# Four chains of sampled attention on one ring of four PSUM banks, next to the banks of the feed-forward

## The chip, the cores and the metric

The kernel runs on one core of a Trainium2 chip. The metric is the device time of one execution in microseconds. Instructions of an engine stand in one queue and start in that order. PE is the engine of the matmuls, PEld its weight loads, DVE, ACT and POOL are the vector, scalar and general engines, and SP issues most of the DMAs. PE writes into PSUM, which has eight banks of 128 x 512 float32.

## What is computed

The reference is a network of four layers on a batch of four sequences of 1024 rows and 128 features. Each layer is an attention-like part and a feed-forward part, each followed by `layernorm(x + part(x))`. The change touches only layer 1:

- *Sampled attention* (16 heads of 8). From 35 sampled keys a measure is worked out for each query, and for each head the 35 queries with the largest measure are *chosen*. Only the chosen queries attend to all 1024 keys, by a softmax. All other rows of the output are the mean of the values. Then the output projection, the residual and the norm.
- *Feed-forward with two routes.* A shared expert for every row, and one of two experts per row by the sign of a gate, each of 128 to 512 to 128 features with a relu. Residual and norm follow.

Layer 2 (linear attention, mixture of experts) starts when layer 1 is done with the last batch.

## The kernel before

The program is written with generators. Each step of a batch (`l1_values`, `l1_chosen`, `l1_project`, `l1_ffn`) is one that yields between groups of instructions, and `weave` (line 52) goes round its generators in turn, one group of each. So the program order interleaves the batches. A scheduler then sets the order of each engine's queue when the program is built, from that program order, from the data and from the free buffers, with a model of time of its own. So the order of PE is fixed at build time, and on the chip a matmul that waits holds up all that stand behind it.

PSUM is handed out by `banks` (line 90). It makes one pool for each tag, with a number of banks; `bank(tag)` gives a function that takes the next tile of that pool. A pool is a ring: with four banks, the fifth tile needs one of the first four to have been read and given back. When the pools are replaced by others (a change of stage), a new pool's banks must have been given back by the old one.

The steps that the change moves, for a batch `b`:

- `l1_choose(1)` (line 574): finds the chosen queries of batches 2 and 3, with two transposes of the measure on PE, and five rounds of maximum (`t`), index search (`iu`) and replacement on DVE, each about 1.2 us. It then writes the indices (`idi`) to DRAM and reads them back as lists (`ix`). `l1_choose(0)` did the same for batches 0 and 1 a stage earlier.
- `l1_values(b)` (line 610): the mean of the values (`pvm`), written to all rows of the output in DRAM (`orows`), and the values themselves (`pv` to `vN`).
- `l1_chosen(b)` (line 637): five indirect DMAs on POOL gather the chosen rows (`xgs`); transposes on PE and two matmuls (`pqs`) make the queries, which DVE masks by head (`qs`). Then a loop of five blocks `j` of 112 queries: scores against 1024 keys in two tiles of 512 (`sc0`, `sc1`); the maximum of each on DVE (`smx`), and a bias from the two (`snm`); two exponentials on ACT with their sums (`esc`); eight transposes of 128 columns into two tiles (`pt`), copied to SBUF by ACT (`eT`); eight matmuls with the values (`pav`); scaling and masking on DVE (`o`); and an indirect DMA on POOL that scatters the block into `orows`. That is five PSUM tiles for each block: two scores, two transposes, one sum.
- `l1_project(b)` (line 744): when all five scatters have landed, SP reads `orows` back (`oL`). Then twice (for each half of the rows): transposes (`pt`), a copy with bias on ACT (`oT`), the output projection (`po`), the residual on DVE (`sp_r`), the norm (`norm_parts`, line 151), and transposes of the normed rows into `xT`.
- `l1_ffn(b)` (line 794): for each half, the gate (`pg`), and for three weights four matmuls with relu (`ph`, by turns on ACT and DVE, to `ht`) and four that add up in one bank (`po<-ht`). It needs `xT` of that half. Each half has 25 matmuls of 512 columns in the program, each of which the profile shows as two instructions. At its end stand a bias on ACT (`yT`), transposes, residual and norm.

`front` orders these. In a first stage it weaves `l1_choose(1)` with the chains of batches 0 and 1 (values, chosen, project). Each of these two chains has a pool of four banks (`c0`, `c1`). Then comes a change of stage: pools `c` (four banks), `f0` (three) and `o0` (one). The chains of batches 2 and 3 share `c`, and beside them goes the feed-forward of batches 0 and 1, one after the other, on `f0` and `o0`. After a second change, the feed-forward of batches 2 and 3 runs on `f0`, `o0`, `f1` and `o1`, and layer 2 follows.

Of the kernel before, what the change touches and what calls it, by code (L numbers as in the profile page):

```python
# [19 lines left out]
B, T, D = 4, 1024, 128  # L20
# [31 lines left out]
def weave(*gens):  # L52

    gens = list(gens)
    while gens:
        for g in gens[:]:
            if next(g, gens) is gens:
                gens.remove(g)


class Net:
# [786 lines left out]
    def front(self, ctx, w0, W, d, dp):  # L848

        tc = self.tc  # L850
        names = lambda n, s: [dp.tile(s, F32, name=f"{n}{b}", bufs=1) for b in range(B)]
        xd, orows = names("xd", [T, D]), names("orows", [T, D])
        ds = [dp.tile([2, 2, HU], I32, name=f"ds{i}", bufs=1) for i in range(2)]
        nb = self.const.tile([P, 4], F32, name="nbz")
        for i in range(2):
            self.nc.vector.tensor_scalar_mul(nb[:, i : i + 1], self.col(f"bz{i}"), -1.0)
            self.nc.vector.tensor_scalar_add(nb[:, 2 + i : 3 + i], self.col(f"bh{i}"), 0.5)
        with ExitStack() as right:
            with ExitStack() as left:
                sp = left.enter_context(tc.tile_pool(name="slot1", bufs=1))  # L860
                wp = left.enter_context(tc.tile_pool(name="slot2", bufs=2))
                with self.banks(g0=2, g1=2, g2=2, g3=2), tc.tile_pool(name="gru", bufs=4) as gp:
                    weave(
                        *(self.l0_gru(b, self.bank(f"g{b}"), self.wgru, nb, gp) for b in range(B))
                    )
                    self.l0_slots(W, sp)
                left.enter_context(self.banks(u=2, p0=3, p1=3))
                pu, pp = self.bank("u"), [self.bank(f"p{b % 2}") for b in range(B)]
                cp = right.enter_context(tc.tile_pool(name="spc", bufs=1, side="right"))
                qp = right.enter_context(tc.tile_pool(name="spq", bufs=2, side="right"))  # L870
                c = self.l1_load(cp)
                c["v"] = {}
                self.l1_gate(cp)
                route = lambda b: self.l0_route(b, pp[b], W, wp)
                read = lambda b, ps: self.l0_read(b, ps, W, wp, xd[b])
                measure = lambda b: self.l1_measure(b, pp[b], c, qp)
                weave(*(route(b) for b in range(B)))
                weave(self.l0_update(pu, W, wp))
                weave(
                    *(chain(read(b, pp[b]), measure(b)) for b in range(2)),  # L880
                    *(read(b, pu) for b in range(2, B)),
                )
                weave(self.l1_choose(0, pu, c, qp, ds[0]), measure(2), measure(3))
            w0.close()
            sp = right.enter_context(tc.tile_pool(name="sp2", bufs=2, side="right"))
            values = lambda b, ps: self.l1_values(b, ps, c, sp, orows[b])
            chosen = lambda b, ps: chain(
                self.l1_chosen(b, ps, c, sp, xd[b]), self.l1_project(b, ps, c, sp)
            )
            with self.banks(c0=4, c1=4):  # L890
                ps = [self.bank(f"c{i}") for i in range(2)]
                weave(
                    self.l1_choose(1, ps[1], c, qp, ds[1]),
                    *(chain(values(b, ps[b]), chosen(b, ps[b])) for b in range(2)),
                )
            fp = ctx.enter_context(tc.tile_pool(name="ff1", bufs=2))
            ffn = lambda b, i: self.l1_ffn(b, self.bank(f"f{i}"), self.bank(f"o{i}"), d, fp)
            with self.banks(c=4, f0=3, o0=1):
                pc = self.bank("c")
                weave(  # L900
                    *(chain(values(b, pc), chosen(b, pc)) for b in range(2, B)),
                    chain(ffn(0, 0), ffn(1, 0)),
                )
        ctx.enter_context(self.banks(f0=3, o0=1, f1=3, o1=1))
        return ffn(2, 0), ffn(3, 1)
# [1309 lines left out]
```

## Time and profile before

| what | us |
| --- | --- |
| median of 17 runs | 2275.1 |
| lowest and highest run | 2268.27, 2285.0 |
| the profiled execution | 2275.47 |
| its span, first to last instruction | 2273.7 |
| PE busy in the span | 1991.2 (88%) |
| DVE, ACT, POOL busy | 1351.0, 1194.1, 1024.0 |
| mean granted clock of PE | 0.934 of full speed |

The profile is of one execution. Times in its timeline count from the start of the span. The marks of the stretch that matters here are these starts:

| mark | us |
| --- | --- |
| first `pvm` of batch 0 | 233.48 |
| first gather (`xgs`) of batch 0 | 241.00 |
| first `sc` of batch 0 | 250.79 |
| first exponential of batch 0 | 257.82 |
| end of the last `pav` of batch 1 | 299.8 |
| `pvm` of batches 2 and 3 | 322.48 |
| first `pg` of the feed-forward of batch 0 | 328.50 |
| first `sc` of batch 2 | 332.50 |
| end of the last `pav` of batch 3 | 425.6 |
| first `pg` of the feed-forward of batch 2 | 465.55 |
| first matmuls of layer 2 (`pv<-wE`) | 598.7 |

How to read it: a busy PE is not PE at its peak, since matmuls are pipelined and their ends are modelled. So the start of one instruction to the start of the next says more than a duration. A wait is put down to the instruction that released it. Idle time of an engine that is not the bottleneck costs nothing by itself.

### The profile page before, as it was taken

Reading aid. Unit: us, or ns where it says so; the run is one execution under the profiler, and the core shown is the slowest. Engines: PE = TensorE matmul, PEld = TensorE weight load, DVE = VectorE, ACT = ScalarE, POOL = GpSimd, SP = SyncE. Lnnn points to the kernel's source line nnn. Section 1 sums busy time; section 2 is a strip of 40 time slices with the busy share of each in tenths; the row PEclk is TensorE's granted clock in tenths of the full one; section 3 lists DMA queues with packets and bytes.
Section 4 is the critical chain, followed back from the end, with each engine's and each line's share of the span. In section 5 each row is a group of like instructions: output and inputs, shape, how many; then the busy total and the mean of one; then the engine's idle time right before and its main releaser. Section 6 shows DMA issues by size and latency. Waiting matters only on the chain.

```text
span 2273.7 us, 46313 instructions
## 1 busy us (share of the span) xinstructions
PE 1991.2 (88%) x17788; PEld 1388.1 (61%) x17788; DVE 1351.0 (59%) x3668; ACT 1194.1 (53%) x2606; POOL 1024.0 (45%) x812
## 2 busy tenths in 40 slices
PE   6679889989999999999979876689899989998998
PEld 3456555544477777787868664346565656565666
DVE  7657743443455554655555565686777688776521
ACT  6533344322244444444565556466768786767443
POOL 5100320000123234234143329989798989879400
PEclk9668889989999999999999997899999999999999
DMA  3000110050000010031232066466776676776421
GB/s 107 0 24 15 38 40 1 19 175 0 1 3 2 3 37 24 18 88 41 80 82 83 17 176 210 124 181 193 199 213 178 182 186 187 196 186 180 108 61 51
DMA packets 138555, 211.09 MB, mean 93 GB/s; under 512 B 18596, under 2 KB 75933, under 8 KB 137950
## 3 DMA queue, kind: packets, MB, share of 16 engines
q1 hardware_dynamic: 126190, 173.87, 25.5%
q0 software_dynamic: 12144, 34.26, 7.2%
q8 instruction: 140, 2.29, 0.4%
q14 instruction: 81, 0.66, 0.1%
HBM read 160.29 MB, written 23.16 MB: 81 GB/s over the span
## 4 chain that ended last, share of the span: by engine, by line
PE 44%; DVE 13%; ACT 11%; issue 3%; DMA 2%; POOL 1%; SPq 0%; ACTq 0%; POOLq 0%; DVEq 0%
PE py L129 8%; PE ph L129 7%; PE po L1131 5%; PE pqk L129 5%; PE pa_m L129 4%; DVE db L1859 4%; PE kp_mo L129 3%; PE pr L1201 2%; PE pv L129 2%; PE pys L129 2%; ACT da L1858 1%; PE pt L133 1%; ACT hh L1985 1%; PE kp_mo L133 1%; ACT xN L176 1%
## 5 line engine op out<-in xcount | busy, mean ns | idle before, releaser
L1064 POOL TENSOR_TENSOR qt<-r_q,sb_c_turn 128x256 f32<-128x256 f32 (+1 forms) x256 | 164.6, 663 | 448.9 <-ACT r_q L1056 444.8
L1870 POOL TENSOR_TENSOR hc<-db,cn 128x1024 f32<-128x1024 f32 x128 | 316.3, 2504 | 62.6 <-PE pys L129 41.0
L129 PEld LDWEIGHTS py<-wh,hh 128*128 128x128 f32 x2048 | 252.8, 194 | 82.5 <-issue 46.7
L1854 POOL TENSOR_TENSOR db<-ud,bn 128x1024 f32<-128x1024 f32 x112 | 289.0, 2654 | 12.4 <-issue 9.9
L129 PE MATMUL py<-wh,hh 128*128 128x128 f32 x2048 | 260.2, 278 | 14.7 <-ACT hh L1985 7.1
L129 PE MATMUL ph<-xT,wh 128*128 128x512 f32 x512 | 255.4, 616 | 19.4 <-DVE h_acc L2001 5.1
L1985 ACT ACTIVATE hh<-ph,sb_cols 128x512 f32<-128x512 f32 x256 | 170.7, 681 | 124.4 <-PE ph L129 97.4
L1122 DVE TENSOR_TENSOR a<-pa_m,sb_c_near 128x256 f32<-128x256 f32 x256 | 96.5, 419 | 203.5 <-PE pa_m L129 203.5
L1079 ACT ACTIVATE kN<-kp_mo,sb_c_trig 128x128 f32<-128x128 f32 x448 | 130.2, 372 | 129.9 <-PE kp_mo L133 121.8
L1858 ACT ACTIVATE da<-dl,aneg 128x512 f32<-128x512 f32 x224 | 153.3, 689 | 79.7 <-DVE db L1859 78.8
L129 PE MATMUL pys<-hc,sb_c_ident 128*128 128x512 f32 x324 | 160.7, 626 | 20.3 <-POOL hc L1870 16.7
L1859 DVE TENSOR_TENSOR_SCAN db<-da,carry,db 128x512 f32<-128x512 f32 x128 | 157.1, 1265 | 12.8 <-ACT da L1858 9.9
L1859 DVE TENSOR_TENSOR_SCAN db<-da,db 128x512 f32<-128x512 f32 x128 | 149.3, 1204 | 9.2 <-POOL db L1854 5.2
L129 PEld LDWEIGHTS ph<-xT,wh 128*128 128x128 f32 x512 | 89.3, 195 | 100.4 <-issue 53.5
L2001 DVE SCALAR_TENSOR_TENSOR h_acc<-py,gt,h_acc 128x128 f32<-128x128 f32 x256 | 71.9, 342 | 130.2 <-PE py L129 130.2
L129 PE MATMUL pqk<-xT,wE 128*128 128x256 f32 x512 | 137.5, 392 | 8.3 <-ACT coT L1198 4.3
L129 PEld LDWEIGHTS pys<-hc,sb_c_ident 128*128 128x128 f32 x324 | 61.4, 202 | 83.9 <-issue 57.8
L129 PEld LDWEIGHTS pqk<-xT,wE 128*128 128x128 f32 x512 | 89.2, 194 | 22.0 <-DVE cv L1041 8.1
L1198 ACT COPY coT<-pt 128x512 f32<-128x512 f32 x64 | 37.6, 587 | 118.2 <-PE pt L133 118.2
L129 PE MATMUL po<-ht,wD 128*128 128x512 f32 x192 | 92.5, 594 | 0.0
L844 DVE TENSOR_SCALAR ht<-ph,sb_cols 128x512 f32<-128x512 f32 x48 | 35.7, 749 | 90.2 <-PE ph L129 90.1
L1131 PE MATMUL po<-cv,a 128*64 128x65 f32 x2048 | 88.3, 228 | 0.0
(453 smaller groups left out, 4275.0 us busy)
## 6 DMA issues: line engine op xcount, KB each, us to landing
wx<-in_wF SPq DMA_DIRECT2D x92, 384.0 KB, 3.4
bn<-rows SPq DMA_DIRECT2D x128, 256.0 KB, 4.8
cn<-rows SPq DMA_DIRECT2D x128, 256.0 KB, 4.4
wh<-in_wH SPq DMA_DIRECT2D x64, 512.0 KB, 3.7
hc<-hc POOLq DMA_DIRECT2D x47, 512.0 KB, 7.0
xrows<-zero SPq DMA_DIRECT2D x4, 1472.0 KB, 10.5
xg<-xrows SPq DMA_DIRECT2D x20, 256.0 KB, 3.6
yrows<-ys SPq DMA_DIRECT2D x20, 256.0 KB, 3.2
```

What stands on the lines that cost most here:

```text
L129: return self.nc.tensor.matmul(out=out, lhsT=lhsT, rhs=rhs, start=start, stop=stop)
L133: self.nc.tensor.transpose(out, in_, self.ident[0:n, 0:n])
L1064: nc.gpsimd.tensor_mul(u["qt"][:, m, a:], u["q"][:, a:], c2["turn"][:, m, o + a : o + 2 * P])
L1079: self.nc.scalar.activation(u["kN"][:, c, m, :], pk[:, c, :], AF.Copy, scale=trig[:, k, m : m + 1])
L1122: nc.vector.tensor_mul(u["a"][:, i, :, :], pa[i], self.c2["near"][:, None, :].to_broadcast([P, 2, P]),)
L1131: self.nc.tensor.matmul(out=u["po"][self.HALF[j], i, c, :], lhsT=lhsT, rhs=rhs, start=key not in u["begun"], stop=True, skip_group_check=True,
L1854: nc.gpsimd.tensor_mul(db, ud, bc[0])
L1858: nc.scalar.activation(da, dl[:, ec, :], AF.Exp, scale=aneg[:, j : j + 1])
L1859: nc.vector.tensor_tensor_scan(db[:, ec, :], da, db[:, ec, :], carry[:, ec, n : n + 1] if h else 0.0, ALU.mult, ALU.add,)
L1870: nc.gpsimd.tensor_mul(hc, db, bc[1])
L1985: nc.scalar.activation(ht, ph, AF.Relu, bias=self.col("h_b1", i=e * NK + k))
L2001: nc.vector.scalar_tensor_tensor(acc[:, c, :], py[:, c, :], gt[:, c, e : e + 1], acc[:, c, :], ALU.mult, ALU.add,)
```

## The change

Both stages become one, with the pools `c=4`, `f0=3`, `o0=1` from the start. `chosen_pair(0)` runs the chain of batch 0 and then that of batch 2, and `chosen_pair(1)` the chains of batches 1 and 3. `l1_choose(1)` and both pairs take all their PSUM tiles from the one ring `c`. When a chain has been written out to its end, its batch is put into `ready`, and `ffn_pair` begins with the feed-forward of a batch when it finds it there. The last stage is as it was.

```diff
-            with self.banks(c0=4, c1=4):
-                ps = [self.bank(f"c{i}") for i in range(2)]
-                weave(
-                    self.l1_choose(1, ps[1], c, qp, ds[1]),
-                    *(chain(values(b, ps[b]), chosen(b, ps[b])) for b in range(2)),
-                )
             fp = ctx.enter_context(tc.tile_pool(name="ff1", bufs=2))
             ffn = lambda b, i: self.l1_ffn(b, self.bank(f"f{i}"), self.bank(f"o{i}"), d, fp)
+            ready = set()
+
+            def chosen_pair(b):
+
+                for b in (b, b + 2):
+                    yield from values(b, pc)
+                    yield from chosen(b, pc)
+                    ready.add(b)
+
+            def ffn_pair():
+
+                for b in range(2):
+                    while b not in ready:
+                        yield
+                    yield from ffn(b, 0)
+
             with self.banks(c=4, f0=3, o0=1):
                 pc = self.bank("c")
                 weave(
-                    *(chain(values(b, pc), chosen(b, pc)) for b in range(2, B)),
-                    chain(ffn(0, 0), ffn(1, 0)),
+                    self.l1_choose(1, pc, c, qp, ds[1]),
+                    chosen_pair(0),
+                    chosen_pair(1),
+                    ffn_pair(),
                 )
```

## The prediction

> **What bounds the kernel now.** I read the page first: PE is busy for 88% of the span. The change touches one stretch of 232 us, so next I cut that stretch into parts with the view of busy time by window: the loop of chains 0 and 1 (257.8 to 299.8), their projection and the change of banks (to 328.5), the loop of chains 2 and 3 (332.5 to 425.6), and their projection (to 465.5). The columns are length, then busy time (and count) of PE, PEld, DVE, ACT, POOL, then the granted clock.
>
> ```profile
> 257.80:299.80 42.00, 40.74 (x276) 29.77 (x276) 26.05 (x77) 23.43 (x60) 17.71 (x19) 1.00 0.10 16
> 299.80:328.50 28.70, 18.08 (x113) 15.46 (x113) 12.49 (x58) 10.64 (x22) 5.81 (x4) 0.76 0.27 74
> 332.50:425.60 93.10, 90.00 (x388) 53.65 (x387) 38.00 (x111) 38.75 (x80) 8.47 (x9) 0.93 0.01 1
> 425.60:465.50 39.90, 33.29 (x123) 18.13 (x121) 20.07 (x79) 11.54 (x21) 0.94 (x1) 0.93 0.10 27
> ```
>
> The reader is to see that PE bounds the first loop and the third part, and that the second part is the hole: 10.6 of 28.7 us without PE work, at a clock of 0.76. The view of waits for PE in that part names the longest:
>
> ```profile
> PE pt L133 <- DMA oL<-orows: 5.4, 1, 5.4
> ```
>
> Third, the timeline of PE in the first loop, where each chain has four banks (start, length, what; the idle time before it in brackets):
>
> ```profile
> 279.14 1.95 PE L129 MATMUL sc<-kT,qs 128*112 128x512 f32 x4
> 280.93 0.93 PE L133 MATMUL pt<-sb_c_ident,esc 112*128 112x112 f32 x8
> 281.70 1.67 PE L129 MATMUL pav<-vN,eT 128*112 128x32 f32 x16
> 283.20 1.95 PE L129 MATMUL sc<-kT,qs 128*112 128x512 f32 x4
> 284.99 0.88 PE L129 MATMUL pav<-vN,eT 128*112 128x32 f32 x8
> 285.71 0.96 PE L133 MATMUL pt<-sb_c_ident,esc 112*128 112x112 f32 x8
> 286.91 0.97 PE L129 MATMUL pav<-vN,eT 128*112 128x32 f32 x8 [0.24 <-ACT eT L712]
> 287.72 1.95 PE L129 MATMUL sc<-kT,qs 128*112 128x512 f32 x4
> ```
>
> Scores (sc) of one chain stand between the transposes (pt) and sums (pav) of the other: the chains are half a round apart, and each one's softmax hides behind the other's matmuls. A round of both takes 287.72 - 279.14 = 8.6 us with 0.24 us idle.
>
> Fourth, the timeline of the loop of chains 2 and 3, which already share one ring of four. This round has almost no feed-forward work in it:
>
> ```profile
> 413.22 2.81 PE L129 MATMUL sc<-kT,qs 128*112 128x512 f32 x6
> ...
> 416.24 0.69 ACT L695 ACTIVATE esc<-sc,snm 112x512 f32<-112x512 f32 x1 [3.64 <-DVE snm L691]
> ...
> 419.11 0.69 ACT L695 ACTIVATE esc<-sc,snm 112x512 f32<-112x512 f32 x1 [0.19 <-DVE ln_mv L161]
> ...
> 419.94 1.27 PE L133 MATMUL pt<-sb_c_ident,esc 112*128 112x112 f32 x8 [1.59 <-ACT esc L695]
> ```
>
> Here both chains run in step: all scores first, then both wait for the exponentials, the second chain's 2.87 us after the first's.
>
> **The change, part by part.** Each queue's order in the changed program, as built, shows the same instructions but two more ACT table loads (2531 ACT instructions for 2529). What changes is order, and five terms follow.
>
> **1. The loop of chains 0 and 1, +13 us.** Ten tiles a round (two sc, two pt, one pav a chain) on four banks force the in-step order: in the changed order PE has sc A, sc A, sc B, sc B, pt A x2, pt B x2, pav A, pav B. Work of a round from the rows above: four sc at 0.44 x 2, four pt at 0.39, two pav at 1.5, or 8.1 us. Waits, with sc A's start as 0: the first maximum starts 1.13 later (279.14 to 280.27 in the trace), the second maximum is late because the rest of the last pav B now stands between the two sc A, so exp A starts at about 4.0; pt A may follow an exponential by 1.0 (258.50 to 259.52), at 5.05, while PE is free at 4.25: 0.8 idle. On DVE the row for chain B's bias is behind chain A's sum of exponentials, so exp B starts at about 6.45 and pt B at 7.45, with PE free at 6.1: 1.35. Two waits of 0.3 for second halves are left. 8.1 + 2.75 = 10.8 us a round. The measured in-step rounds agree: 358.70 to 370.50 is 11.8 with 0.86 of feed-forward and 0.43 of yT transposes in it, so 10.5.
>
> The start is later as well. PE now has chain 0's pqs behind the fourth gathered block of chain 1, which it transposes at 253.73; before, pqs ran at 247.77. On DVE the choice of batches 2 and 3 goes ahead of most of qs: pqs at 254.0, qs 0.69 later, then a maximum 1.22, two qs 0.5 each, an index search 1.28, a qs, and two reductions with small casts between, which brings the first exponential to about 261.5 for 257.82. Since exp A is 4.0 into a round, round 1 counts from 257.5. The last pav ends at 257.5 + 4 x 10.8 + 12 = 312.7, against 299.8: +13. Bounds: +2 if a round stays at 8.57, +26 if it takes 13.5, as it would with PE at half clock in half of it (sc pairs then take 1.92 instead of 1.02).
>
> POOL now has the ten gathers for chains 2 and 3 ahead of all scatters. They wait for the choice, which now ends near 261 (at 268.83 before), with 4.3 from there to the first gather (268.86 to 273.12) and 12.4 for ten. The scatters start at about 278; the first buffer of four is wanted again in the third round, past 286. I cost this at nothing.
>
> **2. The first projection, -4 us.** The wait of 5.4 for oL stays: nothing in PE's new order stands in it. The first xT is copied at 314.75, 15 us after the last pav; there the feed-forward (pg, ph) now starts, instead of 28.7 us after it. But values, gathered blocks and pqs of chains 2 and 3 are put behind almost its whole first half. From the last pav to chain 2's first sc: before 32.7 us with 3 feed-forward matmuls at 0.86 in them, 30.1 without. After, 15.7, then 25 such matmuls (21.5), the values (3.9), the transposes and pqs (3.0) and 3.5 left of the projection: 47.6, or 26.1 without the 21.5. So -4; bounds -11 (all 10.6 idle filled) and 0.
>
> **3. The loop of chains 2 and 3, +1 us.** 50 feed-forward matmuls instead of 47, paid for in terms 2 and 4. Two rounds are unfilled in either order. The two table loads of 1.28, and exp of chain 3 behind a square root that waits for the feed-forward's statistics, give 0 to +4; I take 1.
>
> **4. The second projection, +8.5 us.** This is what is late next. Before, a half of feed-forward (25 x 0.86 = 21.5) runs inside 39.9 us, so the rest costs 18.4. In the new order the feed-forward of batch 1 has ended its first half before the first oL transpose, and its next half stands behind the whole projection. The cover is gone, and the chain scatter, oL, transpose, po, two normalisations runs bare, as the first one did: there the last xT was copied 26.3 us after the last pav, though values were in between (pv 3.74). I take 27: 27 - 18.4 = +8.5. Bounds 0 and +12.
>
> **5. Later layers, 0.** Up to the expert layers the order is the same; in the last layer some pairs swap. No row prices that; I allow 4 us either way, three scans of 1.27.
>
> Sum: 13 - 4 + 1 + 8.5 = +18.5. The profiled execution took 2275.47 us (span 2273.7, 1.8 outside it), and the median of 17 runs is 2275.1, so the same holds for both: **2294 us**.
>
> [...] After the waits of 1.30 and 1.59 us PE slowed (second view, a pair of sc at 1.92):
>
> ```profile
> 365.92 1.27 PE L133 MATMUL pt<-sb_c_ident,esc 112*128 112x112 f32 x8 [1.30 <-ACT esc L695]
> ...
> 370.50 1.92 PE L129 MATMUL sc<-kT,qs 128*112 128x512 f32 x2
> ```
>
> The granted clock was 0.57 from 370 to 380 us and 0.66 from 420 to 430. In the first loop, with waits of 0.24, it was 1.00. [...] By the rows the new loop may lose the clock in each round, up to the +26 of term 1 and a sum of +31.
>
> **Rivals.**
> - *The loop also loses its clock* (13.5 us a round): 26 - 4 + 1 + 8.5 = +31.5, 2307 us. For it: both unfilled in-step rounds were followed by a low clock. Against: sc rows recur every 11 us. 0.20.
> - *Faster*: the feed-forward fills the first hole entirely and the ring costs the loop nothing, since a bank comes free before PE reaches it. Then +2 - 11 + 1 + 3 (a tail half covered): -5, 2270 us. It decides at a round of 8.9 us or less. For it: ACT is busy for 23.4 and DVE for 26.0 of 42 us, so no other engine forces a longer round. Against: the measured in-step rounds. 0.08.
> - *Nothing to see*: rounds of 9.5 (+6), the hole half filled (-7), a tail at +3 and 1: +3, 2278. The holes only change places. 0.10.
> - The forecast: 2282 to 2303 us, 0.62.
>
> **How the numbers follow.** About 0.2%, 4.5 us, is what a measurement of this kernel can tell from no change. Faster by more than that: 0.08; within it: 0.10; slower: 0.62 + 0.20 = 0.82. The range leaves out the faster rival and the upper half of the clock rival: 2277 to 2309.
>
> **What would show it.** Right: in-step order in the first loop with PE waits for exp of 1 us or more, the last pav of chain 1 near 313, ph starting some 16 us after it, no ph between chain 3's last pav and its last xT, and the first pg of batch 2 near 484 instead of 465.55. Wrong: rounds under 9 us, or ph inside the second projection. A changed time in the layers after 620 us would have another cause.

## The result and the profile after

The changed kernel took 2306.5 us (median of 8 runs, 2301.82 to 2311.12); the kernel before took 2275.87 (46 runs). The ratio is 1.0132, interval 1.0115 to 1.0148: 30.6 us slower. The profiled execution took 2315.62 us (span 2313.8), 9 us above the median; a second profiled execution of the changed kernel, taken with the experiments, took 2299.06, 7 below it. Both are used here, as *changed* and *changed again*.

Busy time by window of the changed kernel, with the columns of the prediction's first fence (length, PE, PEld, DVE, ACT, POOL, clock, DMA share, GB/s): the first loop, the first projection, the feed-forward that now stands between, the second loop, the second projection.

```profile
260.70:323.70 63.00, 56.88 (x281) 38.83 (x279) 23.65 (x73) 24.35 (x61) 17.82 (x19) 0.79 0.07 11
323.70:343.10 19.40, 8.52 (x41) 7.46 (x42) 6.20 (x30) 4.73 (x8) 0.94 (x1) 0.59 0.19 56
343.10:375.40 32.30, 32.30 (x130) 19.03 (x130) 14.77 (x39) 12.13 (x24) 4.69 (x2) 0.96 0.12 33
375.40:466.60 91.20, 87.94 (x396) 50.89 (x394) 40.03 (x114) 39.04 (x82) 8.47 (x9) 0.98 0.01 2
466.60:493.90 27.30, 14.68 (x72) 11.83 (x71) 14.29 (x70) 8.36 (x15) 0.94 (x1) 0.78 0.13 36
```

The first loop is longer by 14 us (63.0, where 250.8 to 299.8 was 49.0), and most of that is *busy* time: PE is busy for 56.9 us with fewer instructions (281, where 290 took 45.5), because its clock was 0.79 and not 0.99. The same stretch before:

```profile
250.80:299.80 49.00, 45.51 (x290) 31.83 (x288) 33.01 (x90) 25.50 (x63) 19.68 (x22) 0.99 0.10 17
```

The last row of the changed kernel's is the second projection without feed-forward: PE works for 14.7 of 27.3 us.

The timeline of PE in the first loop shows both. Columns: start, length, what, and in brackets the idle time before.

```profile
274.38 1.27 PE L133 MATMUL pt<-sb_c_ident,esc 112*128 112x112 f32 x8 [0.19 <-ACT esc L695]
276.28 1.27 PE L133 MATMUL pt<-sb_c_ident,esc 112*128 112x112 f32 x8 [0.63 <-ACT esc L695]
277.39 2.46 PE L129 MATMUL pav<-vN,eT 128*112 128x32 f32 x24
279.68 1.09 PE L129 MATMUL sc<-kT,qs 128*112 128x512 f32 x2
...
284.60 1.27 PE L133 MATMUL pt<-sb_c_ident,esc 112*128 112x112 f32 x8 [0.46 <-ACT esc L695]
286.51 1.38 PE L133 MATMUL pt<-sb_c_ident,esc 112*128 112x112 f32 x8 [0.64 <-ACT esc L695]
287.68 4.55 PE L129 MATMUL pav<-vN,eT 128*112 128x32 f32 x24
292.05 2.03 PE L129 MATMUL sc<-kT,qs 128*112 128x512 f32 x2
```

Both chains' transposes stand together, each behind an exponential: the in-step order. Up to 287 the waits are only 0.19 to 0.64 us and a round takes 9.0 to 9.9 (the first sc pair of a round to the next, 260.71, 269.74, 279.68). At 287.7 the same 24 sums take 4.55 for 2.46, and a pair of scores 2.03 for 1.09: PE is at half clock, where it was 1.00 from 260.7 on. The next rounds take 12.4, 14.0 and, to the end of the last sums, 17.9. The clock over them: 0.55 from 287.7 to 299, 1.00 to 303, 0.50 from 306 to 314.

Executions differ ahead of this stretch by some microseconds (the first `pvm` of batch 0 came at 233.48, 235.97 and 230.82 us in these three), so I count from there:

| from first pvm | before | changed | changed again |
| --- | --- | --- | --- |
| to the first exponential | 24.3 | 27.6 | 27.5 |
| from there to the last pav of batch 1 | 42.0 | 60.3 | 54.4 |
| to the first sc of batch 2 | 32.7 | 51.6 | 50.9 |
| to the last pav of batch 3 | 93.1 | 91.3 | 92.5 |
| to the first pg of batch 2 | 39.9 | 27.2 | 27.7 |
| sum | 232.1 | 258.0 | 253.0 |
| from there to the end of the span | 1808.1 | 1819.9 | 1813.5 |

The front of the change costs 20.9 to 25.9 us, and what follows the first `pg` of batch 2 (1808.1 for the kernel before) costs 5.4 to 11.8 more. Below, the *front* is the stretch from the first `pvm` to that `pg`, and the *rest* is what follows.

### The profile page after: what moved, and what is told of

It reads as the page before. It is cut to its first block, busy times and chain, and to the rows that moved or that the text cites. A ratio compares the mean times of both kernels' runs of the same rounds, so it can differ in the third digit from the quotient of the medians.

```text
span 2313.8 us, 46346 instructions
## 1 busy us (share of the span) xinstructions
PE 2008.3 (87%) x17788; PEld 1399.5 (60%) x17788; DVE 1356.5 (59%) x3668; ACT 1196.1 (52%) x2608; POOL 1024.0 (44%) x812
## 4 chain that ended last, share of the span: by engine, by line
PE 40%; DVE 13%; ACT 10%; issue 4%; POOL 2%; DMA 2%; SPq 0%; POOLq 0%; ACTq 0%; DVEq 0%
PE py L129 7%; PE ph L129 6%; PE po L1143 5%; DVE db L1871 5%; PE pqk L129 5%; PE pa_m L129 4%; PE kp_mo L129 2%; PE pv L129 2%; PE pr L1213 2%; PE pys L129 2%; ACT hh L1997 1%; PE pt L133 1%; ACT da L1870 1%; PE kp_mo L133 1%; POOL db L1866 1%
## 5 line engine op out<-in xcount | busy, mean ns | idle before, releaser
L129 PE MATMUL pa_m<-r_q,r_k 64*64 64x128 f32 x2048 | 87.2, 286 | 0.1
## 6 DMA issues: line engine op xcount, KB each, us to landing
xrows<-zero SPq DMA_DIRECT2D x4, 1472.0 KB, 10.2
```

Source lines behind the costliest of these rows:

```text
L129: return self.nc.tensor.matmul(out=out, lhsT=lhsT, rhs=rhs, start=start, stop=stop)
```

## The experiments

Three groups of four kernels ran, each on a chip of its own with runs of the kernel before beside them, which took 2278.0, 2278.7 and 2316.3 us in the three groups. So groups are compared by ratios. Each kernel has one profiled execution, which can lie some microseconds off its median.

| run | us | ratio to before | interval |
| --- | --- | --- | --- |
| ring8_in_step | 2319.0 | 1.0179 | 1.0131 to 1.0227 |
| ring4_offset | 2281.5 | 1.0008 | 0.9991 to 1.0024 |
| filler_in_loop | 2308.4 | 1.0141 | 1.0111 to 1.0171 |
| choose_later | 2319.2 | 1.0176 | 1.0146 to 1.0206 |
| ring4_stage_kept | 2295.5 | 1.0083 | 1.0056 to 1.0110 |
| changed_again | 2308.7 | 1.0148 | 1.0129 to 1.0166 |
| offset_and_cover | 2275.3 | 0.9992 | 0.9974 to 1.0010 |
| two_rings_of_two | 2269.0 | 0.9963 | 0.9949 to 0.9977 |
| late_order_of_before | 2337.7 | 1.0083 | 1.0065 to 1.0102 |
| late_order_of_ring8 | 2339.1 | 1.0087 | 1.0067 to 1.0108 |
| two_rings_cover | 2308.8 | 0.9974 | 0.9958 to 0.9991 |
| two_rings_choose_apart | 2305.2 | 0.9949 | 0.9929 to 0.9968 |

My theory was that four banks for ten tiles a round force the in-step order. The rivals: the order comes from the weave and one shared ring, however many banks it has; and the loss is mostly clock.

### Is it the four banks?

`ring8_in_step`, on the kernel before:

```diff
-            with self.banks(c0=4, c1=4):
-                ps = [self.bank(f"c{i}") for i in range(2)]
+            with self.banks(c=8):
+                ps = [self.bank("c")] * 2
```

> The kernel before, with its change of stage, but chains 0 and 1 and the second choice take their tiles from one ring of eight banks (c=8) and not from two rings of four. PE's order, as built, then has both chains' scores first, then both chains' transposes, as in the changed kernel. Ring theory (my prediction: four banks for ten tiles a round make the loop slow): eight banks are enough, so the loop takes the 49 us from first sc to last pav that it took before, and the run 2276 us, within 5. In-step theory (two chains that are woven group for group and start together stay together, whatever the number of banks): PE waits for esc by 0.5 us or more in each round, the loop takes 55 to 63 us, and the run 2283 to 2298 us. Clock theory (most of the loss is clock that PE loses after such waits): the same 2283 to 2298, with sc pairs of 1.9 us and over in part of the loop.

The loop took 58.6 us and the run 2319.0, above the range of every theory. Its timeline:

```profile
286.33 1.11 PE L133 MATMUL pt<-sb_c_ident,esc 112*128 112x112 f32 x8
288.76 1.27 PE L133 MATMUL pt<-sb_c_ident,esc 112*128 112x112 f32 x8 [1.31 <-ACT esc L695]
289.87 2.46 PE L129 MATMUL pav<-vN,eT 128*112 128x32 f32 x24
292.16 1.95 PE L129 MATMUL sc<-kT,qs 128*112 128x512 f32 x4
293.94 0.88 PE L129 MATMUL pav<-vN,eT 128*112 128x32 f32 x8
294.66 1.95 PE L129 MATMUL sc<-kT,qs 128*112 128x512 f32 x4
296.45 0.98 PE L133 MATMUL pt<-sb_c_ident,esc 112*128 112x112 f32 x8
```

With twice the banks the chains are in step all the same, PE waits 1.31 us for the second chain's exponential, and a round takes 296.45 - 286.33 = 10.1 us. My step "ten tiles a round on four banks force the in-step order" falls. The front took 248.7, 16.6 over before, and the rest 1830.0 for 1808.1: there its order differs too.

`ring4_offset`, on the changed kernel:

```diff
-                    chosen_pair(1),
+                    chain([None] * 1, chosen_pair(1)),
```

> The changed kernel with one edit: the pair of chains 1 and 3 starts one round of the weave later. Ring of four, one stage and all else stay. PE's order, as built, has the scores of one chain between the transposes and the sums of the other. Ring theory: four banks are still too few, PE waits for them or for exponentials as in the changed kernel, loop of 60 us or more, 2303 to 2310 us. In-step theory: rounds of 8.6 to 9.5 us, loop of 45 to 50 us from first sc to last pav, and 12 to 18 us off the changed kernel: 2288 to 2295 us; the second projection stays bare, with the first pg of batch 2 about 27 us after the last pav. Clock theory: the same, with the clock at 1.00 through the loop.

Measured 2281.5: 25 us off the changed kernel, on the same four banks. PE in its loop:

```profile
272.28 1.88 PE L129 MATMUL sc<-kT,qs 128*112 128x512 f32 x4
274.00 1.67 PE L129 MATMUL pav<-vN,eT 128*112 128x32 f32 x16
276.07 1.27 PE L133 MATMUL pt<-sb_c_ident,esc 112*128 112x112 f32 x8 [0.40 <-ACT esc L695]
277.18 1.88 PE L129 MATMUL sc<-kT,qs 128*112 128x512 f32 x4
```

One chain's scores and sums stand between the other's exponentials and transposes. The waits are 0.40, four scores take 1.88 in each row from 262 to 302 (those at 254.15 took 3.62), and two half rounds take 2 x 4.9 = 9.8 us. That is hardly less than the 9.9 of the in-step rounds of the changed kernel ahead of 287.7, and more than I expected (8.6 to 9.5). The clock over the loop is 0.93, where the changed kernel's was 0.79 and 0.88. So in this loop the order saves the clock more than it saves waits. Not all of the 25 us is the loop's: in its profiled execution (2289.8, the slowest of ten) the front took 242.3, 10.7 to 15.7 less than the changed kernel's, and the rest 1810.2, 3.3 to 9.7 less, with an order of its own there.

`two_rings_of_two`, on the changed kernel:

```diff
             def chosen_pair(b):
+                pc = self.bank(f"c{b}")
...
-            with self.banks(c=4, f0=3, o0=1):
-                pc = self.bank("c")
+            with self.banks(c0=2, c1=2, f0=3, o0=1):
...
-                    self.l1_choose(1, pc, c, qp, ds[1]),
+                    self.l1_choose(1, self.bank("c1"), c, qp, ds[1]),
```

> The changed kernel with the four banks split in two rings of two (c0=2, c1=2), one for each pair of chains; the second choice is on the ring of the second pair. As built, the chains' halves alternate on PE, and the order from layer 2 on is nearly that of the kernel before. Ring theory: two banks for the five tiles of a block make each chain wait for its own copies and exponentials, rounds of 11 us and more, loop of 60 us or more, 2305 us or more. In-step theory: the chains are not in step, rounds of 9 to 10 us at full clock, loop of 50 to 55 us, 2280 to 2290 us.

```profile
277.99 1.09 PE L129 MATMUL sc<-kT,qs 128*112 128x512 f32 x2
278.91 0.55 PE L133 MATMUL pt<-sb_c_ident,esc 112*128 112x112 f32 x4
279.30 1.03 PE L129 MATMUL sc<-kT,qs 128*112 128x512 f32 x2
280.16 0.55 PE L133 MATMUL pt<-sb_c_ident,esc 112*128 112x112 f32 x4
280.55 1.76 PE L129 MATMUL pav<-vN,eT 128*112 128x32 f32 x16
...
286.29 1.09 PE L129 MATMUL sc<-kT,qs 128*112 128x512 f32 x2
```

In these rows PE never waits (in the whole loop four times, by 0.4 us at most), and a round of both chains takes 286.29 - 277.99 = 8.3 us, less than the 8.6 on eight banks before. At 2269.0 us it beats both kernels (0.9963 of before). Two rings of two banks do what one ring of four, or of eight, doesn't.

`two_rings_choose_apart` takes two_rings_of_two and moves away what else might hold the chains apart, the choice on the second ring:

```diff
-                    self.l1_choose(1, self.bank("c1"), c, qp, ds[1]),
+                    self.l1_choose(1, self.bank("f0"), c, qp, ds[1]),
```

> two_rings_of_two with the second choice on a feed-forward bank and not on the ring of chains 1 and 3, so that nothing but the weave sets the chains against each other. If the chains are out of step only because the choice holds chain 1 back: in step, rounds of 10 us, 2280 us or more. If two rings of their own are enough, since only a shared ring hands out its banks in the weave's order: rounds of 8.3 to 9 us, 2265 to 2273 us.

```profile
291.05 1.95 PE L129 MATMUL sc<-kT,qs 128*112 128x512 f32 x4
...
299.67 1.95 PE L129 MATMUL sc<-kT,qs 128*112 128x512 f32 x4
```

A round takes 299.67 - 291.05 = 8.6 us. The ratio is 0.9949 (the 2305.2 us are those of the slower third group): rings of their own are enough. The built orders name the reason. A ring hands out its banks in the program's order, and in the program the weave alternates the two chains group by group; on one ring a chain's next tile comes behind the other chain's tile of the same group. On rings of their own the scheduler is free to set them half a round apart. This is read from the built orders and the rounds, and no run shows the handing out itself.

### Is it the clock?

`filler_in_loop`, on the changed kernel (the result of the added matmul is read by nothing):

```diff
+            if b < 2 and j:
+                fill = self.bank("f0")([JR, 256], "fill")
+                self.mm(fill, eT[:, NC - 1, :], kT[:, 0:256])
             yield
             rs = wp.tile([JR, 1], F32, name="srs")
```

> The changed kernel with eight more matmuls of 256 columns in the loop of chains 0 and 1 (one for each chain and block from the second on), into a feed-forward bank, with a result that nothing reads. They are extra work, 8 x 0.44 = 3.5 us at full clock. Clock theory: PE's gaps get shorter, the clock stays at 1.00 for longer, the loop ends 8 to 11 us earlier than at 323.7 in spite of the extra work, 2296 to 2300 us. If the lost clock doesn't come from PE's waits, or if it costs little: 3 us more than the changed kernel, 2309 us.

```profile
296.98 1.09 PE L129 MATMUL sc<-kT,qs 128*112 128x512 f32 x2
...
305.30 5.89 PE L129 MATMUL pav<-vN,eT 128*112 128x32 f32 x32
```

The clock held nearly to the end: a pair of scores takes 1.09 in every round, also in the last (296.98), only the last sums are slow (5.89), and the clock over the loop is 0.95. The last pav came 80.4 us after the first pvm, against 87.9 (changed) and 81.9 (changed again): with 3.5 us of added matmuls, up to 7.5 us earlier. But the whole took 2308.4, the same as the changed kernel: the expected 2296 to 2300 failed. Its front to the first pg of batch 2 took 250.4, 2.6 to 7.6 less than the changed kernel's; the rest took 1822.0, 2.1 to 8.5 more. The traces show why the two can't be told apart by the total: from layer 2 on each engine of this kernel has, but for a few instructions, the order of ring8_in_step and not of the changed kernel. So the filler changed two things. For the clock alone the changed kernel's own executions say more: two of them, with one order, differ by 5.9 us in this loop (`changed_again`, next), and the shorter one lost the clock too.

`changed_again`, without an edit:

> The changed kernel unchanged, for a second profile. Median 2306 us within 3. If its loop always loses the clock: last pav of chain 1 at 320 us or later again, with sc pairs of 2 us in rounds 3 to 5. If that was a chance of the one profiled execution (which took 2315.6 us, 9 above the median): last pav near 311 to 314, sc pairs of 1.1 us, and layer 2 starting near 616 to 620.

Its loop lost the clock later, in the last two rounds only: at 293.58 the 24 sums take 4.55, at 282.33 they took 2.46, and the clock over the loop is 0.88. Rounds, from the first sc pair (255.41): 9.0, 9.95, 10.2, then 13.3 and 14.8. So one and the same program differs by 60.3 - 54.4 = 5.9 us in this loop. ACT, DVE and PE of this execution, where it begins:

```profile
289.11 0.68 ACT L695 ACTIVATE esc<-sc,snm 112x512 f32<-112x512 f32 x1
...
291.20 0.69 ACT L695 ACTIVATE esc<-sc,snm 112x512 f32<-112x512 f32 x1
```

```profile
289.91 0.16 DVE L705 TENSOR_TENSOR srs<-ssum 112x1 f32<-112x1 f32 x1 [0.96 <-ACT esc L695]
290.10 0.17 DVE L706 RECIPROCAL srs<-srs 112x1 f32<-112x1 f32 x1
290.18 0.67 DVE L688 TENSOR_REDUCE smx<-sc 112x1 f32<-112x512 f32 x1
290.89 0.21 DVE L691 TENSOR_SCALAR snm<-smx 112x1 f32<-112x1 f32 x1
```

```profile
292.03 1.75 PE L133 MATMUL pt<-sb_c_ident,esc 112*128 112x112 f32 x8 [1.50 <-ACT esc L695]
293.58 4.55 PE L129 MATMUL pav<-vN,eT 128*112 128x32 f32 x24
```

In rounds 4 and 5 DVE has chain B's second maximum and bias behind chain A's sum (srs), which waits for ACT; so B's exponential is late (291.20) and PE waits 1.50. In round 3 the maximum stands ahead of that sum and only the bias behind it:

```profile
278.88 0.69 DVE L688 TENSOR_REDUCE smx<-sc 112x1 f32<-112x512 f32 x1 [0.17 <-PE sc L129]
279.96 0.16 DVE L705 TENSOR_TENSOR srs<-ssum 112x1 f32<-112x1 f32 x1 [0.39 <-ACT esc L695]
280.04 0.21 DVE L691 TENSOR_SCALAR snm<-smx 112x1 f32<-112x1 f32 x1
```

Rounds 1 and 2 have the same order, and in all three PE waits about 0.64 for chain B. The prediction named this queue and priced the wait at 1.35 in every round; that size comes in rounds 4 and 5 alone.

### Where does the rest go?

`choose_later`:

```diff
-                    self.l1_choose(1, pc, c, qp, ds[1]),
                     chosen_pair(0),
                     chosen_pair(1),
+                    chain([None] * 6, self.l1_choose(1, pc, c, qp, ds[1])),
```

> The changed kernel with the second choice (batches 2 and 3) started six rounds of the weave later, behind both chains in the weave. DVE then has the queries of chains 0 and 1 (qs) ahead of the choice. If the late start of the loop (first sc at 260.7 for 250.8) comes from the choice's maxima and searches ahead of qs: first sc near 252 to 255, and 5 to 8 us off the changed kernel, 2298 to 2301 us; the gathers of batches 2 and 3 come later, at no cost, since they are wanted only after the projection. If the start is set by something else (gathers, transposes): no change, 2304 to 2309 us. If the choice now stands among the maxima of the loop and takes from it what it gave at the start: also no change, with longer rounds 2 to 4.

A miss: 2319.2, 12.7 more than the changed kernel. The first sc came 26.6 us after the first pvm (24.7 changed), so the choice was not what held it. In both kernels PE's first pqs stands right behind the ninth gathered block, which it transposes at 256.20 in the changed kernel and at 257.38 here:

```profile
256.20 0.42 PE L133 MATMUL pt<-sb_c_ident,xgs 112*128 112x112 f32 x1 [0.84 <-DMA xgs<-xd,ix]
256.41 3.04 PE L129 MATMUL pqs<-xsel,sb_w_sp 128*128 128x280 f32 x6
```

These are lines of the changed kernel. In choose_later DVE had the choice in the loop, though the loop got no longer:

```profile
261.86:323.80 61.94, 55.51 (x289) 37.53 (x287) 38.72 (x96) 25.31 (x63) 17.89 (x19) 0.83 0.07 11
```

The front took 259.8 us, 1.8 to 6.8 over the changed kernel's, and the rest 1823.0, again with an order of its own.

`ring4_stage_kept`, on the kernel before, separates front from rest, since its order from layer 2 on is that of the kernel before:

```diff
-            with self.banks(c0=4, c1=4):
-                ps = [self.bank(f"c{i}") for i in range(2)]
+            with self.banks(x=4, c=4):
+                ps = [self.bank("c")] * 2
```

> The kernel before, with its two stages, but in the first stage chains 0, 1 and the second choice take their tiles from one ring of four banks (the other four are left empty). As built, PE's order in the first loop is that of the changed kernel, the feed-forward runs in the first projection and not in the second, also as there, and the order from layer 2 on is that of the kernel before on every engine. If all of the changed kernel's loss arises before layer 2 (28.4 us in its profiled execution, 598.7 to 627.1): 2301 to 2306 us, the same as the changed kernel. If part of it comes from the other order of the later layers (the profiled execution has 11.7 us more there): less than the changed kernel by that part, 2294 to 2300 us. If the loss comes from the merged stage and not from the ring and the step: 2276 us.

Its front is that of the changed kernel's first profile almost to the microsecond: 87.8 to the last pav, 257.6 to the first pg of batch 2. (Keeping the stage didn't hold the feed-forward back: its banks take the place of the four empty ones.) So the ring and its order explain the front, and the merged stage adds nothing that shows there. The median is 2295.5, 13 us below changed_again in the same group; its profiled execution was the slowest of five. The rest took 1812.0, 3.9 over the kernel before with the same order.

`late_order_of_before` and `late_order_of_ring8`, on the changed kernel, leave the front alone and change the order behind it:

```diff
-        return ffn(2, 0), ffn(3, 1)
+        return chain([None] * 2, ffn(2, 0)), ffn(3, 1)
```

```diff
-        return ffn(2, 0), ffn(3, 1)
+        return ffn(2, 0), chain([None] * 3, ffn(3, 1))
```

> The changed kernel with one edit at the end of layer 1: the feed-forward of batch 2 starts two rounds of its weave later. As built, the chains and both projections keep the changed kernel's order; from layer 2 on VectorE, ScalarE and GpSimd have the order of the kernel before. If the later layers' other order is part of the loss (ring4_stage_kept, with the order of the kernel before there, took 2295.5 us, 11 to 13 less than the changed kernel): 2294 to 2300 us, and 8 us or more below late_order_of_ring8. If all of the loss is ahead of layer 2: 2304 to 2309 us, as the changed kernel.

> The changed kernel with the feed-forward of batch 3 started three rounds of its weave later. As built, the chains and both projections keep the changed kernel's order; from layer 2 on the order is that of ring8_in_step, whose profiled execution took 22 us more from layer 2 to the last expert matmul than the kernel before (1688.0 for 1666.2). If the later layers' order makes that difference: 10 to 22 us more than late_order_of_before, 2308 to 2320 us. If it was chance: the same as late_order_of_before, within 4 us.

The ratios are 1.0083 and 1.0087. The first fits with ring4_stage_kept (1.0083 too) and lies below the changed kernel (1.0132 and 1.0148): with the order of the kernel before behind the front, the loss would be 0.8% and not 1.4%. But the second was to cost 10 to 22 us more and cost 1.3, inside its interval. So "the order of before is cheap and that of ring8_in_step dear" isn't shown by the times. In this group all four profiled executions have PE waits that no record explains. These are two of them, in the first loop of late_order_of_before:

```profile
276.81 1.68 PE L133 MATMUL pt<-sb_c_ident,esc 112*128 112x112 f32 x8 [1.85 <-issue]
284.03 1.76 PE L133 MATMUL pt<-sb_c_ident,esc 112*128 112x112 f32 x8 [5.55 <-issue]
```

They go on through the whole span. Those over 0.2 us that are put down to issue sum to 36.3 us in late_order_of_before, 20.7 in late_order_of_ring8, 28.4 and 29.9 in the other two, and there is none in the ten profiles from outside this group. So this pair differs in them by more than the effect that it was to show. The rest, by the order from layer 2 on (as the traces show it, the same or nearly so within a row):

| order of the rest | profiled executions, us |
| --- | --- |
| of the kernel before | 1808.1 (before), 1812.0 (ring4_stage_kept) |
| of the changed kernel | 1819.9, 1813.5 |
| of ring8_in_step | 1830.0 (itself), 1822.0 (filler_in_loop) |
| third group, of before | 1838.8, of it 28.5 such waits: 1810.3 without |
| third group, of ring8_in_step | 1843.0, of it 18.4 such waits: 1824.6 without |

The last two figures are estimates, since a wait that is taken off may have hidden another. By these rows the three orders keep their rank; by the medians of the pair they do not. The changed kernel itself wasn't run in the third group, so how much of its 30.6 us is due to the order of the later layers stays open: its profiled executions say 5.4 and 11.8 us by the table above, where two executions of one order differ by 4 to 8, and the ratios say 11 to 15.

### Is the bare second projection worth its price?

`offset_and_cover` is ring4_offset with the feed-forward two rounds later:

```diff
                     while b not in ready:
                         yield
+                    if b == 0:
+                        yield from [None] * 2
                     yield from ffn(b, 0)
```

> The changed kernel with the pair of chains 1 and 3 one round of the weave later (as in ring4_offset, 2281.5 us) and the feed-forward two rounds later. As built, half a feed-forward moves from the loop of chains 2 and 3 into their projection, and the loop of chains 2 and 3 keeps its half-round order. By term 4 of the prediction a bare second projection costs 8.5 us (28.0 us bare in ring4_offset, for 18.4 credited): 5 to 9 us off ring4_offset, 2272 to 2277 us. If the cover is worth nothing, or if the loop of chains 2 and 3 needs the feed-forward as a filler for its waits as much as the projection does: 2280 to 2284 us.

The feed-forward now runs inside the second projection:

```profile
442.70 1.06 PE L133 MATMUL pt<-sb_c_ident,oL 128*128 128x128 f32 x4
443.56 0.90 PE L133 MATMUL pt<-sb_c_ident,xN 128*128 128x128 f32 x4
444.29 1.02 PE L129 MATMUL pg<-xT,gate_d 128*128 128x512 f32 x2
445.15 1.02 PE L129 MATMUL ph<-xT,wD 128*128 128x512 f32 x2
```

2275.3 us and a ratio of 0.9992, against 1.0008: 6 us by the medians, 3.6 by the ratios, with intervals that overlap and in two groups. `two_rings_cover`, the same edit on two_rings_of_two, gained nothing (0.9974 against 0.9963):

> two_rings_of_two (2269.0 us) with the feed-forward started two rounds later. As built, half a feed-forward moves from the loop of chains 2 and 3 to the last third of the second projection and beyond. By term 4, part of the bare projection (26.3 us there) is covered: up to 4 us less, 2265 us. If the loop of chains 2 and 3 needs its filler more, or since the cover comes only after the last output projection (po): no gain or a loss, 2269 to 2277 us.

There the feed-forward comes only after the last output projection. A cover seems to be worth about half of what term 4 charges for its loss; that the loop gives up what the projection gains is a guess, and by these intervals even the half is not certain.

## Why the prediction was right, and where it was not

The direction held and the measured 2306.5 us lies in the range of 2277 to 2309, but 12 us above the forecast of 2294 (+30.6 for +18.5), and above the 2282 to 2303 of the main forecast. That it lies inside is in part luck: the cause given for the order was wrong, and what the sum put at nothing, the clock in the loop and the later layers, happened to end below the upper bound. By its terms, as measured in the two profiled executions of the changed kernel (each by its own differences to before):

| term | forecast | changed | changed again |
| --- | --- | --- | --- |
| 1 loop of chains 0 and 1, with its start | +13 | +21.6 | +15.6 |
| 2 first projection | -4 | -0.1 | -0.8 |
| 3 loop of chains 2 and 3 | +1 | -4.4 | -3.2 |
| 4 second projection | +8.5 | +8.8 | +9.3 |
| sum of the front | +18.5 | +25.9 | +20.9 |
| 5 later layers | 0 | +11.8 | +5.4 |

For term 2, 22 feed-forward matmuls at 0.86 are taken off that moved into it, as the prediction did; for term 3, the 3 more of them that it holds; for term 4, the 25 that left are credited.

- **Term 1 was mis-sized, and its reason was wrong.** The first exponential came 3.2 us later, as worked out (3.7). The in-step rounds at full clock took 9.0 to 10.2 us, less than the 10.8 forecast. What was missing is the clock, lost in the last two or three rounds, which then took 12.4 to 17.9. That the waits would cost no clock, as the sum has it, no row of before shows; the runs show 0.79 and 0.88 over this loop, and 1.00 in ring8_in_step from 284.7 to 309.8 through waits of 1.30 to 1.40. The sum came out too low by 3 to 9 us. And the step "ten tiles a round on four banks force the in-step order" failed: eight banks on one ring give that order too, four banks with one chain a step later do not, and four in two rings give rounds of 8.3.
- **The clock rival** said +26 for this term and 2307 us in all. The total was met by chance, the term was not (15.6 to 21.6); the rest of the total came from behind the front. Its estimate, half of each round at half clock, fits neither execution: two or three rounds at 9.0 to 10.2 us come first, then three or two of 12.4 to 17.9.
- **Term 2 was too hopeful.** The prediction had one wait for oL, and the feed-forward some 16 us after the last pav. PE waited twice for oL and once more for the norm, and the first ph came 20.9 and 20.6 us after the last pav. The waits of the changed kernel, in total, times and longest:

```profile
PE pt L133 <- DMA oL<-orows: 7.6, 2, 4.3
PE pt L133 <- DVE xN L180: 3.2, 1, 3.2
```

- **Term 3** was on the other side by 4 to 5 us. In the second loop the mean clock went from 0.93 to 0.98: it fell once, near 383 to 387 (0.57), where before it fell twice, near 368 to 378 (0.51) and at the end (0.76 from 420 to 425.6). In the second profile the rows from 371.5 to 377 are the slow ones, with a pair of ph at 1.91 for 1.02.
- **Term 4 held**: no ph between chain 3's last pav and its last xT, and 27.2 and 27.7 us to the first pg of batch 2, where 27 was forecast.
- **Term 5 was wrong.** "No row prices that; I allow 4 us" was the weakest step, and the term measures 5.4 and 11.8 us, where two executions of one order differ by 4 to 8. How the pairs in the later layers cost it is not settled.
- **The faster rival** was to decide at a round of 8.9 us or less with the ring free of cost. The changed kernel's first round took 9.0 and then the rounds grew. It does happen when the ring is cut in two: 8.3 us, and 2269.0.

On the clock the rows do not agree on one cause. ring8_in_step lost its clock at a wait of 3.24 us at the start of its loop:

```profile
261.68 3.17 PE L133 MATMUL pt<-sb_c_ident,esc 112*128 112x112 f32 x16 [3.24 <-ACT esc L695]
264.64 6.05 PE L129 MATMUL pav<-vN,eT 128*112 128x32 f32 x32
```

Here 32 sums take 6.05 and the eight scores after them 6.24; at the end of the loop 32 sums take 3.24, and in the changed kernel's first round eight scores took 3.60. At 279.75, behind a wait of 1.14, 24 sums take 2.46 again, and the clock was 1.00 from 284.7 to 309.8, through waits of 1.31, 1.30 and 1.40. The changed kernel lost it at 287.7 after waits of 0.46 and 0.64, and no wait since the start of its loop was longer. So a wait of 3.24 us stood ahead of one fall and none above 0.64 ahead of the other, and what sets the clock in these loops stays open.

## What to carry to other kernels

When two chains of work are woven together, look at how their buffers are handed out before counting them: here one shared ring went with the weave's in-step order (ratios of 1.0132 with four banks and 1.0179 with eight), and two rings of two banks of their own beat both (0.9963). An edit that lets a pipeline start one step later costs nothing to write and helps to tell whether an order or a resource is the bound. And where an order is planned for the whole program, a change at its front moves the order far behind it; that part of the time deserves a term and a range of its own.

## What the runs showed that was not expected

- One program's loop took 60.3 and 54.4 us in two executions, by the round in which PE fell to half clock; waits as short as 0.46 and 0.64 us stood before one fall, while ring8_in_step showed no fall in four rounds with waits of 1.14 to 1.40.
- In the last group, on a chip of its own, each of the four kernels shows PE waits put down to issue, 20.7 to 36.3 us in the whole span, which the other ten profiles don't have, and the kernel before took 2316.3 us there for 2278.
